# Causal attention steps of tiles 5+0, 4+1, 3+2, 6, 7, with both tiles of a step transposed by one VectorE instruction in two of three causal layers

## The chip, the cores and the metric

The kernel runs on one core of a Trainium2 chip. Five compute engines work beside each other, each with its own instruction stream: TensorE (PE, matrix products, with its weight loads shown apart as PEld), VectorE (DVE), ScalarE (ACT), GpSimd (POOL) and SyncE (SP), which here issues DMAs. They meet through semaphores; a wait at the head of an engine's stream holds everything behind it. TensorE writes to PSUM, a small memory of accumulators; the other data lies in SBUF, 128 partitions wide. The metric is the device time of one execution in microseconds, the median of several runs. A query tile is 128 rows.

## The reference, cut to what matters

Four transformer layers on x of 2 x 1024 x 128, each an attention and a feed-forward part with a layer norm ahead and a residual sum behind. All attentions have 16 heads of 64. Layer a has one key and value head shared by all and no mask; b, c and d are causal; c's keys and values come from a latent of 32 numbers per position; d has biases on its projections.

```python
def _L0_attn_b_ref(x, w_q, w_k, w_v, w_o):            # layer b; c and d alike but for what is said above
    q = jnp.einsum('bsd,hqd->bhsq', x, w_q)
    k = jnp.einsum('bsd,hqd->bhsq', x, w_k)
    v = jnp.einsum('bsd,hvd->bhsv', x, w_v)
    scores = jnp.einsum('bhsq,bhtq->bhst', q, k)
    causal = jnp.triu(jnp.ones((s, s), dtype=bool), k=1)
    masked = jnp.where(causal, -jnp.inf, scores)
    weights = jax.nn.softmax(masked / jnp.sqrt(jnp.float32(dq)), axis=-1)
    out = jnp.einsum('bhst,bhtv->bhsv', weights, v)
    cat = out.transpose(0, 2, 1, 3).reshape(b, s, -1)
    return jnp.einsum('bsf,df->bsd', cat, w_o)

x = x + attn_a(ln(x)); x = x + ffn(ln(x))             # ffn of a and b: dense, weight quantized to 6 bits
x = x + attn_b(ln(x)); x = x + ffn(ln(x))
x = x + attn_c(ln(x)); x = x + moe(ln(x))             # moe of c and d: top 2 of 8 experts, and a shared one
x = x + attn_d(ln(x)); x = x + moe(ln(x))
```

## The kernel before

**Units and steps.** The attention of a layer is cut into 16 units: a batch entry (2) and a pair of heads (8). A unit's 1024 queries are 8 tiles of 128 (NT). A step computes the scores of both heads for one query tile, or for two whose keys together fill the eight key tiles. In layer a a unit has 8 steps of one tile. In a causal layer tile qt has qt + 1 key tiles, and a unit has five steps, `CAUSAL_STEPS` (L588): [7], [6, 0], [5, 1], [4, 2], [3], of 8, 8, 8, 8 and 4 key tiles. So layer a has 128 steps, and b, c and d have 80 each. All steps of all units run one after another in one loop; the feed-forward parts, layer norms and the next unit's projections are cut in small parts and strewn between the steps.

**What one turn of the loop issues, in order.** The order on every engine is that of the text, written out by hand. For step s:

1. `transposes` (L764) for step s-2, the normalized probabilities of which are now ready. Before its second part, `normalize` (L702) for step s-1: DVE takes the reciprocals of the sums (L704), POOL multiplies (L708).
2. `add_products`: POOL adds finished output products to x (L894).
3. `scores` for step s: PE products into two PSUM tiles of two banks, one per head (L638), with the causal mask added by PE (L644 in b and d, L653 in c); DVE takes the negated row maxima (L682). `exponentials`: ACT, with the sums (L697). The two PSUM tiles are all there are, so a head's scores wait until ACT has read the same head's scores of the step before.
4. Copies queued by the transposes (ACT, L1146), then `out_product` (L864): PE's product with the output weights (L871) and ACT's copy out of PSUM (L878).
5. Parts of the next unit's projections (L533, L556, L571, their ACT copies, L541 in layer c, and in b and d the DMAs that swap the halves of q and k, L516) and of the side work.
6. `release` and `weigh_some(4)`: PE's products of up to four key tiles of transposed probabilities with the values (`weigh`, L850; c: L845, L841). They go into one PSUM tile `av` (the only one of its kind). When a bank of query tiles ends, ACT copies it to `attnT` (L861; d: L857).

**Two ways to transpose.** The products with the values need the probabilities with the keys on the partitions. The query tiles are taken in pairs, qb = qt // 2. In the first way (tiles 4 to 7 of a causal layer, and the first seven key tiles of all tiles in a) DVE transposes 32 x 32 blocks in place in each partition group (L778, STREAM_TRANSPOSE) from `pr` into `slots`. When both tiles of a pair are there, `blocks_moved` (L739) moves the sixteen blocks [quarter i of partitions, quarter r] of `slots` to their places in `prT`: 16 DMAs from SP's queue (L753); in layer a the diagonal ones need only change their place inside their own partitions and are copied, quarters 1 and 2 by POOL (L757) and 3 by ACT. In the second way (tiles 0 to 3 of the causal layers, the last key tile in a) PE transposes tiles of 128 x 128 into a PSUM tile `pp` of four (L794, from the pool `ps_m` of three buffers, which the projections and output products use too), and ACT copies them to SBUF (L795).

**Homes.** The transposed probabilities of a pair lie in a home: `prT_many[0]`, `prT_many[1]` or `prT_four` by their number of key tiles. `prT_of` (L713) takes it, and if products of an earlier pair that lies there are still to be issued, it issues them at once, at that place in the order. A pair becomes `ready` two steps after it was moved, or at once if PE transposed it; ready pairs are weighed in the order of `BANKS` (L590), in a causal layer [3], [0, 1], [2] (pairs), so a unit ends three banks.

Of the kernel before, what the change touches and what calls it, by code (L numbers as in the profile page):

```python
# [9 lines left out]
F32 = mybir.dt.float32  # L10
# [7 lines left out]
P = 128  # L18
B, S, D = 2, 1024, 128
NT = S // P  # L20
# [12 lines left out]
SCALE = 1.0 / 8.0  # L33


@with_exitstack
def kernel(ctx: ExitStack, tc: tile.TileContext, a: dict, out: bass.AP):
# [30 lines left out]
    def load_attn(names):  # L68
# [33 lines left out]
    slots = probTp.tile([P, 2, 2 * NT * AB], F32, tag="slots", name="slots")  # L102
    prT_many = [
        probTp.tile([P, 2 * NT * AB], F32, tag=f"prT{n}", name=f"prT{n}") for n in range(2)
    ]
    prT_four = probTp.tile([P, 2 * 4 * AB], F32, tag="prT_four", name="prT_four")
# [472 lines left out]
    def tag_of(u):  # L579
# [8 lines left out]
    CAUSAL_STEPS = [[7], [6, 0], [5, 1], [4, 2], [3]]  # L588

    BANKS = {  # L590
        "shared": [[0, 1], [2, 3]], "full": [[3], [0, 1], [2]], "latent": [[3], [0, 1], [2]],
        "bias": [[3], [0, 1], [2]],
    }

    BLOCKED = {"shared": (0, 1, 2, 3), "full": (2, 3), "latent": (2, 3), "bias": (2, 3)}
    HOMES = {8: "first", 6: "second", 4: "four", 2: "rest"}
    probT, pv_of, held = {}, {}, {}
# [4 lines left out]
    def blocked(u, qb):  # L602

        if qb not in BLOCKED[layers[u[0]]["kind"]]:
            return 0
        nk = keys(u, qb * TPA + TPA - 1)
        return nk if layers[u[0]]["causal"] else nk - 1
# [4 lines left out]
    def step_of(u, qts):  # L612
        k = f"{tag_of(u)}_{qts[0]}"
        at = {}
        if len(qts) == 2:
            at = {qts[1]: 0, qts[0]: keys(u, qts[1]) * P}
        else:
            at = {qts[0]: QB - min(QB, keys(u, qts[0]) * P // 2)}
        pr = probp.tile([P, NT, 2, P], F32, tag="pr", name=f"pr_{k}")
        tot = small.tile([P, 2, len(qts)], F32, tag="tot", name=f"tot_{k}")  # L620
        return dict(u=u, qts=qts, at=at, k=k, pr=pr, tot=tot)
# [66 lines left out]
    def tiles_of(st, qt):  # L688
        t0 = st["at"][qt] // P
        return st["pr"][:, t0 : t0 + keys(st["u"], qt)]  # L690
# [22 lines left out]
    def prT_of(u, qb):  # L713


        nk = keys(u, qb * TPA + TPA - 1)
        odd = nk == NT and qb % 2 and not layers[u[0]]["causal"]
        for part in ("second", "rest") if odd else (HOMES[nk],):
            old, held[part] = held.get(part), (u, qb)
            while old:  # L720
                if any(x[:2] == old for x in products):
                    weigh_some(4)
                elif any(x["key"] == old for x in late):
                    release()
                else:
                    break
        if odd:
            return prT_many[1]
        return {
            8: prT_many[0], 6: prT_many[1][:, : 12 * AB], 4: prT_four, 2: prT_many[1][:, 12 * AB :]  # L730
        }[nk]

    def blocks_of(u, qb):

        return slots[:, 1 - qb % 2, : 2 * blocked(u, qb) * AB]

    def blocks_moved(u, qb):  # L739


        t, src = prT_of(u, qb)[:, : 2 * blocked(u, qb) * AB], blocks_of(u, qb)
        n = src.shape[1] // 4
# [3 lines left out]


        copied = (1, 2, 3) if layers[u[0]]["kind"] == "shared" else ()
# [12 lines left out]
        probT[u, qb] = t.rearrange("p (i t k h q) -> p t h i k q", t=TPA, h=2, i=4, q=32)  # L762

    def transposes(st):  # L764

        u = st["u"]
        for qt in st["qts"]:
            qb, cols = qt // TPA, slice(qt % TPA * P, (qt % TPA + 1) * P)  # L770
            nk, nb = keys(u, qt), blocked(u, qb)
            tiles = tiles_of(st, qt)
            if nb:
                n = min(nk, nb)
                dst = blocks_of(u, qb).rearrange(
                    "p (r t c q) -> p t c r q", r=4, t=TPA, q=32
                )[:, qt % TPA, : 2 * n]
                nc.vector.transpose(  # L778
                    dst,
                    tiles[:, :n].rearrange("p k h (r q) -> p (k h) r q", q=32),  # L780
                )
                yield
            if nb < nk and nb:
                o = rest_of(u, qb)[:, qt % TPA].unsqueeze(2)
            elif nb < nk:
                if (u, qb) not in probT:
                    probT[u, qb] = prT_of(u, qb).rearrange("p (h k q) -> p h k q", h=2, q=AB)
                o = probT[u, qb][:, :, :, cols]
            for k0 in range(nb, nk, 2):
                k1 = min(k0 + 2, nk)  # L790
                pt = ps_m.tile([P, 2, 2, P], F32, tag="pm", name=f"pp_{tag_of(u)}_{qt}_{k0}")
                for h in range(2):
                    for kt in range(k0, k1):
                        nc.tensor.transpose(pt[:, h, kt - k0, :], tiles[:, kt, h, :], ident)  # L794
                nc.scalar.copy(o[:, :, k0 - nb : k1 - nb], pt[:, :, : k1 - k0, :])  # L795
                yield
            complete[u, qb] = complete.get((u, qb), 0) + 1
            if nb and complete[u, qb] == TPA:
                blocks_moved(u, qb)

    def rest_of(u, qb):

        held["four"] = u, qb
        return prT_four.rearrange("p (n t h q) -> p n t h q", t=TPA, h=2, q=P)[:, qb]

    def weigh(u, qb, bank, kt, ends):
# [11 lines left out]

        def moving(h, kt, t0, t1=TPA):
            if not blocked(u, qb):  # L820
                return probT[u, qb][:, h, kt, t0 * P : t1 * P]
            if kt >= blocked(u, qb):
                return rest_of(u, qb)[:, :, h]
            x = probT[u, qb][:, t0, h] if t1 - t0 == 1 else probT[u, qb][:, :, h]
            return x[:, :, kt] if t1 - t0 == 1 else x[:, :, :, kt]

        def shaped(o, t0, t1=TPA):
            if not blocked(u, qb):
                return o[:, t0 * P : t1 * P]
            if kt >= blocked(u, qb):  # L830
                return o.rearrange("p (t q) -> p t q", t=TPA)
            if t1 - t0 == 1:
                return o[:, t0 * P : t1 * P].rearrange("p (i q) -> p i q", q=32)
            return o.rearrange("p (t i q) -> p t i q", t=TPA, q=32)

        for h in range(2):
# [12 lines left out]
            else:  # L849
                nc.tensor.matmul(  # L850
                    shaped(av[ROWS[h], n], t0), lhsT=vs[u][:, kt, h, :], rhs=moving(h, kt, t0),
                    start=(kt == 0), stop=(kt == nkt - 1),
                )
# [110 lines left out]
    late = deque()  # L964
# [66 lines left out]


    nc.gpsimd.memset(slots[:, 0, 2 * (NT - 1) * AB :], 0.0)
# [56 lines left out]
    for step, (n, u, qts, i, total) in enumerate([*steps, *[(None, None, None, 0, 1)] * 4]):  # L1090
# [31 lines left out]
        if st:  # L1122
# [6 lines left out]
            for qb in {qt // TPA for qt in st["qts"]}:  # L1129
                if complete[st["u"], qb] == TPA:  # L1130
                    x = next(x for x in late if x["key"] == (st["u"], qb))
                    x["ready"] = step + (2 if blocked(st["u"], qb) else 0)
# [101 lines left out]
```

## Time and profile before

| | us |
|---|---|
| median of 3 runs (2292.64 to 2297.32) | 2293.26 |
| the profiled execution | 2291.09 |
| its span, from the first to the last recorded instruction | 2289.4 |
| PE busy | 2103.5 (92%) |
| DVE busy | 1691.4 (74%) |
| ACT busy | 1492.9 (65%) |
| POOL busy | 1294.1 (57%) |
| bytes moved by DMA | 320 MB, 140 GB/s on average |

The profile is one execution on the chip. An engine's busy time is the union of its instructions; PE's matrix products are pipelined, so the durations of single ones add up to more than their union, and a group's own busy time is given apart from the mean duration of one. A line of a group reads: line of the kernel, engine, operation, output <- inputs by the program's names, shapes and count; then the busy microseconds and the mean nanoseconds of one; then the idle time of the engine just before these instructions, and which engine's instruction ended it. The mean granted clock of TensorE in this execution was 0.971 of full speed. The four layers follow each other along the span, each with the feed-forward part of the layer before strewn into its steps, and the last feed-forward part stands alone at the end.

### The profile page before, as it was taken

Reading aid. Unit: us, or ns where it says so; the run is one execution under the profiler, and the core shown is the slowest. Engines: PE = TensorE matmul, PEld = TensorE weight load, DVE = VectorE, ACT = ScalarE, POOL = GpSimd, SP = SyncE. Lnnn points to the kernel's source line nnn. Section 1 sums busy time; section 2 is a strip of 40 time slices with the busy share of each in tenths; the row PEclk is TensorE's granted clock in tenths of the full one; section 3 lists DMA queues with packets and bytes.
Section 4 is the critical chain, followed back from the end, with each engine's and each line's share of the span. In section 5 each row is a group of like instructions: output and inputs, shape, how many; then the busy total and the mean of one; then the engine's idle time right before and its main releaser. Section 6 shows DMA issues by size and latency. Waiting matters only on the chain.

```text
span 2289.4 us, 43111 instructions
## 1 busy us (share of the span) xinstructions
PE 2103.5 (92%) x14833; PEld 1231.8 (54%) x14833; DVE 1691.4 (74%) x2375; ACT 1492.9 (65%) x3340; POOL 1294.1 (57%) x1723
## 2 busy tenths in 40 slices
PE   6999999999998999999997888888889999999986
PEld 2454444444445666666654444444455666656663
DVE  7978999999886876678668877766766656766544
ACT  5777777667865666666655566655666557666652
POOL 4757777668765555465546655555644446544441
PEclk9999999999999999999998899999999999999998
DMA  5666666556676666666655556644665556646450
GB/s 140 145 150 155 159 154 149 131 131 150 153 189 152 149 160 162 161 155 154 147 131 124 129 130 139 141 109 103 171 157 133 122 119 158 161 118 145 111 139 10
DMA packets 144632, 320.42 MB, mean 140 GB/s; under 512 B 48288, under 2 KB 58784, under 8 KB 144416
## 3 DMA queue, kind: packets, MB, share of 16 engines
q1 hardware_dynamic: 144416, 317.67, 58.8%
q8 instruction: 120, 1.97, 0.4%
q14 instruction: 96, 0.79, 0.1%
HBM read 10.27 MB, written 2.10 MB: 5 GB/s over the span
## 4 chain that ended last, share of the span: by engine, by line
PE 58%; DVE 12%; SPq 9%; POOL 6%; ACT 5%; DMA 5%; issue 5%; DVEq 0%; ACTq 0%; POOLq 0%
SPq L753 9%; PE sc_a L638 7%; PE av_a L850 7%; PE av_d L850 5%; PE sc_b L638 5%; PE av_b L850 4%; PE sc_d L638 4%; DVE slots L778 4%; DMA prT<-slots 4%; ACT pr_c L697 2%; PE sc_c L638 2%; POOL pr_a L708 2%; DVE nmax_d L682 2%; DVE nmax_c L682 2%; PE pp_d L794 2%
## 5 line engine op out<-in xcount | busy, mean ns | idle before, releaser
L708 POOL TENSOR_SCALAR pr_a<-pr_a,rec_a 128x1024 f32<-128x1024 f32 x256 | 284.1, 1122 | 189.3 <-DVE rec_a L704 183.4
L697 ACT ACTIVATE pr_a<-sc_a,nmax_a 128x1024 f32<-128x1024 f32 x256 | 283.2, 1111 | 162.5 <-DVE nmax_a L682 94.1
L708 POOL TENSOR_SCALAR pr_d<-pr_d,rec_d 128x1024 f32<-128x1024 f32 (+7 forms) x256 | 187.0, 748 | 265.9 <-DVE rec_d L704 265.9
L682 DVE TENSOR_REDUCE nmax_a<-sc_a 128x1 f32<-128x1024 f32 x256 | 300.0, 1212 | 49.7 <-PE sc_a L638 49.6
L708 POOL TENSOR_SCALAR pr_b<-pr_b,rec_b 128x1024 f32<-128x1024 f32 (+7 forms) x256 | 190.0, 760 | 216.0 <-DVE rec_b L704 215.8
L682 DVE TENSOR_REDUCE nmax_d<-sc_d 128x1 f32<-128x1024 f32 (+7 forms) x256 | 177.4, 750 | 173.0 <-PE sc_d L644 172.3
L708 POOL TENSOR_SCALAR pr_c<-pr_c,rec_c 128x1024 f32<-128x1024 f32 (+7 forms) x256 | 188.4, 754 | 195.7 <-DVE rec_c L704 195.7
L697 ACT ACTIVATE pr_c<-sc_c,nmax_c 128x1024 f32<-128x1024 f32 (+7 forms) x256 | 186.5, 739 | 146.2 <-DVE nmax_c L682 118.1
L697 ACT ACTIVATE pr_b<-sc_b,nmax_b 128x1024 f32<-128x1024 f32 (+7 forms) x256 | 186.6, 739 | 142.8 <-DVE nmax_b L682 102.8
L697 ACT ACTIVATE pr_d<-sc_d,nmax_d 128x1024 f32<-128x1024 f32 (+7 forms) x256 | 186.6, 739 | 131.6 <-DVE nmax_d L682 117.6
L778 DVE STREAM_TRANSPOSE slots<-pr_a 128x1792 f32<-128x1792 f32 x128 | 261.0, 2039 | 12.7 <-POOL pr_a L708 8.7
L638 PE MATMUL sc_a<-k_a,q_a 64*128 64x512 f32 x512 | 261.3, 629 | 1.7 <-ACT pr_a L697 1.7
L682 DVE TENSOR_REDUCE nmax_b<-sc_b 128x1 f32<-128x1024 f32 (+7 forms) x256 | 177.1, 749 | 111.6 <-PE sc_b L644 110.6
L638 PE MATMUL sc_a<-k_a,qx_a 64*128 64x512 f32 x512 | 258.6, 629 | 0.0
L682 DVE TENSOR_REDUCE nmax_c<-sc_c 128x1 f32<-128x1024 f32 (+7 forms) x256 | 177.3, 750 | 97.7 <-PE sc_c L653 97.7
L850 PE MATMUL av_a<-prT,v_a 128*64 128x256 f32 x1792 | 223.2, 388 | 3.7 <-DMA prT<-slots 1.4
L850 PEld LDWEIGHTS av_a<-prT,v_a 128*64 128x64 f32 x1792 | 121.1, 137 | 122.7 <-issue 70.2
L638 PE MATMUL sc_d<-k_d,q_d 64*128 64x512 f32 (+3 forms) x416 | 158.9, 494 | 0.3 <-ACT pr_d L697 0.3
L638 PE MATMUL sc_b<-k_b,q_b 64*128 64x512 f32 (+3 forms) x416 | 158.8, 494 | 0.0
L638 PE MATMUL sc_b<-kx_b,qx_b 64*128 64x512 f32 (+3 forms) x416 | 153.3, 488 | 0.1
L638 PE MATMUL sc_d<-kx_d,qx_d 64*128 64x512 f32 (+3 forms) x416 | 153.2, 488 | 0.2
L778 DVE STREAM_TRANSPOSE slots<-pr_b 128x2048 f32<-128x2048 f32 (+1 forms) x64 | 121.8, 1903 | 12.0 <-DMA prT<-slots 8.8
(408 smaller groups left out, 4765.1 us busy)
## 6 DMA issues: line engine op xcount, KB each, us to landing
prT<-slots SPq DMA_DIRECT2D x768, 128.0 KB, 2.3
prT<-slots SPq DMA_DIRECT2D x832, 112.0 KB, 2.2
prT<-slots SPq DMA_DIRECT2D x768, 96.0 KB, 2.1
qx_b<-q_b SPq DMA_DIRECT2D x32, 256.0 KB, 3.6
kx_b<-k_b SPq DMA_DIRECT2D x32, 256.0 KB, 3.6
qx_d<-q_d SPq DMA_DIRECT2D x32, 256.0 KB, 3.7
kx_d<-k_d SPq DMA_DIRECT2D x32, 256.0 KB, 3.5
x<-in_x SPq DMA_DIRECT2D x4, 256.0 KB, 3.8
```

Source lines behind the costliest of these rows:

```text
L638: yield nc.tensor.matmul(sc[h][:, at[qt] + k0 : at[qt] + k1], lhsT=q[r, qt * P : (qt + 1) * P], rhs=kk[r, k0:k1], start=True, stop=not dia ...
L682: nc.vector.tensor_reduce(out=nmax[:, n : n + 1], in_=sc[h][:, c], axis=AX.X, op=ALU.max, negate=True)
L697: nc.scalar.activation(tiles_of(st, qt)[:, :, h, :], sc[:, c].rearrange("p (k q) -> p k q", q=P), AF.Exp, bias=nmax[:, n : n + 1], accum_o ...
L708: nc.gpsimd.tensor_scalar(out=pt, in0=pt, scalar1=rec[:, h, n : n + 1], scalar2=1.0, op0=ALU.mult, op1=ALU.mult,)
L753: nc.sync.dma_start(out=o, in_=x)
L778: nc.vector.transpose(dst, tiles[:, :n].rearrange("p k h (r q) -> p (k h) r q", q=32),)
L794: nc.tensor.transpose(pt[:, h, kt - k0, :], tiles[:, kt, h, :], ident)
L850: nc.tensor.matmul(shaped(av[ROWS[h], n], t0), lhsT=vs[u][:, kt, h, :], rhs=moving(h, kt, t0), start=(kt == 0), stop=(kt == nkt - 1),)
```

## The change

The causal steps become [5, 0], [4, 1], [3, 2], [6], [7], of 7, 7, 7, 7 and 8 key tiles, and the banks of a causal layer [1, 2], [0, 3], two instead of three. A step's tiles now lie at the end of the first score bank and from there on, so that a step of 7 key tiles splits into 3 and 4.

`slots` and `prT` are two tiles each, of 21 and of 15 key-tile blocks (`HELD`). `groups_of` says which query tiles are moved together, and `group_of` finds a tile's group. In a the groups are the pairs, as before. In b and d tiles 1, 4, 0, 5, 2, 3 are group 0 (2+5+1+6+3+4 = 21 blocks) and 6, 7 group 1 (15), all transposed by DVE: the two tiles of a step, which lie beside each other in `pr` and in `slots`, by one instruction. A group is moved when its last tile is there, with 13 DMAs and the diagonal quarters 1 and 2 copied by POOL and 3 by ACT (`COPIED`). In c, tiles 4 and 5 (home 0) and 6 and 7 (home 1) are transposed by DVE, each on its own, and moved with 16 DMAs per pair, none copied; tiles 2, 3 and 0, 1 are transposed by PE into home 0 behind them (`natural`). `claim` takes the place of `prT_of`: in a causal layer it takes a home for a whole unit, and it issues the products that are still open of all that lies there.

Instruction counts, per layer:

| | before | after |
|---|---|---|
| b and d: PE transposes (L794) | 320 | 0 |
| b and d: DVE transposes, columns | 16 each of 2048, 1792, 1536, 1280 | 16 of 2048, 64 of 1792 |
| b and d: DMAs of the move | 512 | 416 |
| b and d: POOL copies of the move | 0 | 32 of 32x1344, 32 of 32x960 |
| b and d: ACT copies of the move | 0 | 16 of 32x1344, 16 of 32x960 |
| b and d: ACT copies of PE's transposes | 96 | 0 |
| c: PE transposes | 320 | 320 |
| c: DMAs of the move, columns | 256 of 1024, 256 of 768 | 256 of 704, 256 of 960 |
| b, c and d: copies of av, and of output products | 48 each | 32 each |

The score products keep their number and their sum of columns. Tile 0's and tile 1's first key block are no longer in an order that one instruction can read, so in b and d `weigh` takes them in two of 128 columns.

```diff
-    slots = probTp.tile([P, 2, 2 * NT * AB], F32, tag="slots", name="slots")
-    prT_many = [
-        probTp.tile([P, 2 * NT * AB], F32, tag=f"prT{n}", name=f"prT{n}") for n in range(2)
-    ]
-    prT_four = probTp.tile([P, 2 * 4 * AB], F32, tag="prT_four", name="prT_four")
+    slots, homes = (
+        [
+            probTp.tile([P, n * 2 * P], F32, tag=f"{what}{m}", name=f"{what}{m}")
+            for m, n in enumerate(HELD)
+        ] for what in ("slots", "prT")
+    )
...
-    CAUSAL_STEPS = [[7], [6, 0], [5, 1], [4, 2], [3]]
+    CAUSAL_STEPS = [[5, 0], [4, 1], [3, 2], [6], [7]]
...
-        "shared": [[0, 1], [2, 3]], "full": [[3], [0, 1], [2]], "latent": [[3], [0, 1], [2]],
-        "bias": [[3], [0, 1], [2]],
+        "shared": [[0, 1], [2, 3]], "full": [[1, 2], [0, 3]], "latent": [[1, 2], [0, 3]],
+        "bias": [[1, 2], [0, 3]],
...
+    def groups_of(kind):
...
+        length = [qt + 1 for qt in range(NT)]
+        if kind == "latent":
+            return [
+                dict(home=home, qts=qts, moved=base is None, len=length, base=base)
+                for home, qts, base in (
+                    (0, (4, 5), None), (1, (6, 7), None), (0, (2, 3), 11), (0, (0, 1), 18)
+                )
+            ]
+        return [
+            dict(home=home, qts=qts, moved=True, len=length)
+            for home, qts in ((0, (1, 4, 0, 5, 2, 3)), (1, (6, 7)))
+        ]
...
+    COPIED = {"shared": (1, 2, 3), "full": (1, 2, 3), "latent": (), "bias": (1, 2, 3)}
...
+    def claim(u, g):
+        key = u, g["home"] if layers[u[0]]["causal"] else g["qts"]
+        if held.get(g["home"], [None])[0] == key:
+            return
+        old = {
+            x for home, (k, qbs) in held.items() for x in qbs
+            if home == g["home"] or layers[u[0]]["causal"] and not layers[k[0][0]]["causal"]
+        }
+        qbs = {
+            qt // TPA for x in GROUPS[layers[u[0]]["kind"]] for qt in x["qts"]
+            if x is g or layers[u[0]]["causal"] and x["home"] == g["home"]
+        }
+        held[g["home"]] = key, {(u, qb) for qb in qbs}
+        while old:
+            if any(x[:2] in old for x in products):
+                weigh_some(4)
+            elif any(x["key"] in old for x in late):
+                release()
+            else:
+                break
...
     def transposes(st):
...
+        gs = [group_of(u, qt) for qt in qts]
+        joint = len(qts) == 2 and gs[0] is gs[1] and gs[0]["moved"]
+        for qt, g in zip(qts, gs):
+            nk, nb = keys(u, qt), g["len"][qt] if g["moved"] else 0
             tiles = tiles_of(st, qt)
+            if nb and not (joint and qt == qts[1]):
+                first = qts[1] if joint else qt
+                n = sum(g["len"][x] for x in qts) if joint else nb
...
+                src = st["pr"][:, st["pos"][first] : st["pos"][first] + n]
+                nc.vector.transpose(dst, src.rearrange("p k h (r q) -> p (k h) r q", q=32))
                 yield
...
             elif nb < nk:
...
+                claim(u, g)
+                o = natural(g)[:, g["at"][qt] : g["at"][qt] + nk]
...
+            count = complete[u, g["qts"]] = complete.get((u, g["qts"]), 0) + 1
+            if count == len(g["qts"]):
+                if g["moved"]:
+                    blocks_moved(u, g)
+                finished.append((u, g))
...
     def weigh(u, qb, bank, kt, ends):
...
+        in_blocks = g["moved"] and kt < g["len"][qb * TPA + TPA - 1]
+        whole = not in_blocks or at[1] > at[0]
...
+                for t in (t0,) if t0 or whole else range(TPA):
+                    ts = (t, TPA if whole else t + 1)
+                    nc.tensor.matmul(
+                        shaped(av[ROWS[h], n], *ts), lhsT=vs[u][:, kt, h, :],
+                        rhs=moving(h, kt, *ts), start=(kt == 0),
+                        stop=(kt == qb * TPA + ts[1] - 1 if causal else kt == nkt - 1),
+                    )
```

## The prediction

> **What bounds the kernel now.** I read first the table of stretches, cut where each layer's first score product starts (a from 21, b from 681, c from 1178, d from 1656, the last ffn from 2209 us); its columns are the stretch's length, each engine's busy time with its instructions, the granted clock and the DMA share.
>
> ```profile
> core 0: us, PE busy (x) PEld busy (x) DVE busy (x) ACT busy (x) POOL busy (x), PEclk, DMA share, GB/s
> 21.00:681.00 660.00, 628.74 (x3694) 303.99 (x3694) 591.74 (x613) 489.31 (x877) 459.89 (x475) 0.99 0.64 149
> 681.00:1178.00 497.00, 478.95 (x3643) 319.14 (x3643) 352.14 (x534) 322.93 (x804) 263.69 (x393) 0.99 0.65 154
> 1178.00:1656.00 478.00, 402.08 (x3306) 224.90 (x3305) 356.09 (x549) 303.03 (x777) 272.84 (x411) 0.93 0.55 130
> 1656.00:2209.00 553.00, 530.13 (x3892) 345.31 (x3893) 350.45 (x545) 352.98 (x843) 273.71 (x405) 1.00 0.58 138
> ```
>
> In b and d TensorE (PE) is busy 96% of the time, and VectorE (DVE) 71% and 63%: a product less there is time less. Layer c is another regime: PE 84%, DVE 74%, nothing full, so its pace is a chain of waits from engine to engine. Layer a, which the change leaves alone, shows both engines near full at once: PE 95%, DVE 90%. Second, the groups of instructions, where the change's own operations stand (count, busy us, mean ns, idle before):
>
> ```profile
> L778 DVE STREAM_TRANSPOSE slots<-pr_a 128x1792 f32<-128x1792 f32 x128 | 261.0, 2039 | 12.7 <-POOL pr_a L708 8.7 <-DMA prT<-slots 1.0 <-issue 0.2
> L778 DVE STREAM_TRANSPOSE slots<-pr_b 128x2048 f32<-128x2048 f32 x16 | 36.9, 2306 | 8.8 <-DMA prT<-slots 8.6
> L778 DVE STREAM_TRANSPOSE slots<-pr_b 128x1792 f32<-128x1792 f32 x16 | 32.5, 2033 | 0.3 <-POOL pr_b L708 0.2
> L778 DVE STREAM_TRANSPOSE slots<-pr_b 128x1536 f32<-128x1536 f32 x16 | 28.3, 1770 | 0.5 <-DMA prT<-slots 0.2 <-DMA kx_b<-k_b 0.2
> L778 DVE STREAM_TRANSPOSE slots<-pr_b 128x1280 f32<-128x1280 f32 x16 | 24.0, 1502 | 2.4 <-POOL pr_b L708 2.4
> L794 PE MATMUL pp_b<-ident,pr_b 128*128 128x128 f32 x320 | 49.6, 284 | 5.9 <-ACT attnT_b L878 3.1 <-POOL pr_b L708 2.6
> L794 PE MATMUL pp_d<-ident,pr_d 128*128 128x128 f32 x320 | 48.8, 284 | 4.3 <-POOL rc_n L328 1.9 <-POOL rc_m L328 1.9 <-POOL lnt_n L143 0.4
> L757 POOL TENSOR_SCALAR prT<-slots 32x896 f32<-32x896 f32 x128 | 121.4, 948 | 9.9
> L1146 ACT COPY prT<-slots 32x896 f32<-32x896 f32 x64 | 59.9, 936 | 1.6
> ```
>
> **Layers b and d: what goes.** All 320 PE transposes of each layer go: 49.6 and 48.8 us of PE's busy time. The score products keep their counts and columns. The attention products (av) get 64 narrow instructions more per layer for 32 wide ones, as tile 0's first key block no longer lies beside tile 1's; the trace holds each as two records, so by its rows (narrow 17.5 us per 180 = 0.097, wide 106.9 per 832 = 0.128) 128 x 0.097 - 64 x 0.128 = 4.2 us, and tiles 0 to 3 are now read in strips of 32, whose wide product averages 395 ns against 379: 2 us at most. I take 6 (0 to 8). PE's work is then 479 - 50 + 6 = 435 in b and 530 - 49 + 6 = 487 in d. Over PE's busy time stands an overhead: 497/479 = 1.04 in b, 553/530 = 1.04 in d, and 660/629 = 1.05 in a, where DVE is as full as it will be here. With a's factor b takes 456 (-41) and d 511 (-42); with their own, 452 and 507. I take a's for b and d's own for d, which keeps more spare DVE time: -41 and -46, -87 in all; from -58 (a third of it lost) to -105 (no added products, and the idle 5.9 and 4.3 before the transposes goes too).
>
> **What comes in its place, and what hides it.** DVE, per unit of five steps: four instructions of 2.04 and one of 2.31 for 2.31 + 2.03 + 1.77 + 1.50: 10.46 - 7.61 = 2.85 us more, 45.6 per layer, so 398 of 456 (87%) in b and 396 of 507 (78%) in d. A step of b then has 4.97 us of DVE in 5.7; layer a hides 591.74/128 = 4.62 in 5.16, so I cost it at nothing; without that cover it costs its 45 per layer. POOL gets two copies of 32x1344 and two of 32x960 per unit; at 948/896 ns per column that is 2 x 1.42 + 2 x 1.02 = 4.9 us, 78 per layer: 342 of 456 (75%; a: 70%). ACT loses six copies per unit (at least 26.6 us per layer for the 48 of 128x512) and one pair of output copies, and gets 1.40 + 1.00 us: about even. SyncE (SP) issues 26 DMAs per unit for 32, at some 0.63 us each (its issues in the chain of waits stand 0.6 apart): less. Group 0 is a burst of 13 x 172 KB = 2.2 MB; the fullest stretch of the trace (834 to 842 us) moved 226 GB/s, so 9.9 us and some 2.3 to land. It is issued in a unit's last step, behind the claim of its home, and first read at the end of the next unit's second step, some 14 us on: hidden, by 2 us. Group 1 (1.6 MB, 7.1 us) has as long. If group 0 were 2 us later, PE would wait 2 us per unit, 32 in each layer; one such loss lies within my lower bound of the gain.
>
> [...]
>
> **Layer c: what is moved.** Here tiles 0 to 3 stay with PE, but three things change. Their home is now shared with tiles 4 and 5, and the claim of it, when tile 0 is transposed (ahead of the unit's third scores in PE's order), forces out the products of the previous unit's tiles 0 and 1. These need the one PSUM tile of av, which ACT must empty first, and ACT's copy stands behind the step's exponentials and a projection copy:
>
> ```profile
> 1342.31 0.61 ACT L541 ACTIVATE q_c<-pq_c 128x512 f32<-128x512 f32 x1
> 1342.79 0.39 ACT L861 COPY attnT_c<-av_c 128x256 f32<-128x256 f32 x1
> 1341.15 1.13 PE L638 MATMUL sc_c<-latT,q_c 32*128 32x256 f32 x4 [0.93 <-ACT pr_c L697]
> ```
>
> (Start, duration, instruction, idle before and who ended it.) Before, the next scores start at 1341.15, as soon as the first head's exponentials are read, 1.2 us before ACT is through with the second's (1342.31). After, they wait for that, for 0.6 (q copy), 0.6 (a 128x512 attnT copy: 604 ns), about 0.5 of products (16 take 1.07 in the same timeline) and 0.2 of transposes. That is 3.1 us for the first head and 1.9 for the second; as the second head's scores start late now, I take the mean, 2.5 per unit. Next, the step [3,2] needs 14 PE transposes in four PSUM tiles where the pool has three, so the fourth waits for an ACT copy behind the exponentials; at a 0.6 us copy and the 0.6 it stands behind, 1.2 per unit. On the other side, PE's 27.9 us of waiting for POOL's normalization before these transposes (a row of the groups) came largely from the short step [3] running into the full one [7]; steps are now 7, 7, 7, 7, 8 wide, and I credit two thirds, -1.1 per unit. Sum 2.6 x 16 = +42; bounds 0 (the chain has that slack) and +59 (no credit).
>
> **The end.** The last step was tile 3 with four keys and PE transposes; now it is tile 7 with eight, a DVE transpose, 13 DMAs and their landing with nothing beside them. By 4 more score blocks per head (0.43 us each in nmax and exponentials) and 8 products more I put +4 (0 to +8) on the tail.
>
> **Sum.** 2291.1 (the profiled execution, 2289.4 of it the span) - 87 + 42 + 4 = 2250; the median of the runs stands 2.2 above the profiled execution, so 2252.
>
> **The rivals.** (1) c's chain absorbs the wait, as ACT is idle a third of that layer (303 busy of 478): 2252 - 42 = 2210. Against it: the step's loop passes through ACT's exponentials, and 118 us of ACT's idle is itself a wait in that loop, for the maxima. (2) The other side: DVE sets the pace in b and d. DVE waits 111 us in b and 172 us in d for the scores before it can take their maxima. If these waits stay, because scores wait for a free PSUM pair, which waits for exponentials, which wait for maxima, then the transposes are added in full: b 352 + 46 + 111 + 12 (transposes' own idle) = 521 (+24), d 350 + 46 + 173 = 569 (+16), with c and the tail 2293 + 24 + 16 + 42 + 4 = 2379. It decides as soon as DVE's work and waits pass 6.2 us a step in b and 6.9 in d. Against it: in a the same loop waits only 49.6 us in 128 steps, with more transposing. (3) The removed transposes half stood in gaps: in b's timeline eight records of them take 1.09 us, 0.136 each where the group's mean is 0.155, so some overlap other work; and the gain halves: 2252 + 43 = 2295, no change. Against it: PE's 96%. That the change leaves PE transposes in b and d is excluded by its text: both groups there are marked as moved by DMA.
>
> **How the numbers follow.** Main case 0.60, its own range 2220 to 2284 (b and d from -103 to -72, c from +25 to +58, tail 0 to +8, not all at their ends together). Rival 1 0.17, rival 2 0.13, rival 3 0.10. No change is within 0.2%, 4.6 us, which is about what a measurement of this kernel can tell. The main case and rival 1 are faster; of rival 3 I give 0.03 to faster, 0.04 to same, 0.03 to slower: faster 0.80, same 0.04, slower 0.16. The range takes in rival 1 and most of rival 3, and leaves rival 2 out: 2203 to 2299.
>
> **What would show it.** Right: no pp_b or pp_d group; b's stretch near 456 and d's near 507 with PE still over 93%; the 2.04 us transposes with little idle before them; in c a wait of av_c for ACT of some 2 us, sixteen times, and a stretch near 520. Wrong: DVE over 92% in b with PE's idle before sc_b (rival 2); av_b's first product waiting for prT<-slots by over 1 us per unit (group 0 late); c's stretch still near 478 (rival 1); b and d shortened by half of it with PE as full as before (rival 3).

## The result and the profile after

The changed kernel takes 2310.58 us (median of 4, 2307.93 to 2315.08) where the one before takes 2295.29 beside it: 1.007 times the time, 95% interval 1.0053 to 1.0087. It is slower; a gain of 41 us was forecast. The profiled execution has a span of 2309.2 us against 2289.4. The stretches of the changed kernel, cut as before at each layer's first scores (length, busy time of PE, its weight loads, DVE, ACT, POOL with the instructions, granted clock, DMA share, GB/s):

```profile
21.00:679.00 658.00, 625.22 (x3694) 303.15 (x3694) 590.44 (x610) 488.62 (x876) 458.74 (x475) 0.99 0.64 150
679.00:1158.00 479.00, 447.00 (x3388) 290.74 (x3388) 397.56 (x549) 315.63 (x713) 332.84 (x438) 0.98 0.67 163
1158.00:1685.00 527.00, 420.77 (x3312) 232.96 (x3310) 351.60 (x549) 302.29 (x740) 272.89 (x398) 0.89 0.47 112
1685.00:2221.00 536.00, 501.80 (x3610) 317.35 (x3608) 395.09 (x558) 341.19 (x746) 337.77 (x446) 0.98 0.59 145
2221.00:2309.20 88.20, 56.98 (x296) 35.42 (x293) 36.80 (x101) 21.86 (x36) 23.97 (x20) 0.78 0.20 50
```

| stretch | before | after | change | forecast |
|---|---|---|---|---|
| start and layer a | 681 | 679 | -2 | 0 |
| b | 497 | 479 | -18 | -41 |
| c | 478 | 527 | +49 | +42 |
| d | 553 | 536 | -17 | -46 |
| end | 80.4 | 88.2 | +8 | +4 |

So c lost about what was forecast, and b and d gained 35 us instead of 87. Of b's 49.6 us of PE transposes 32 left PE's busy time, and only 18 the time.

The new operations cost what their rows of before promised. The groups of the transposes in b, and of POOL's copies in d:

```profile
L810 DVE STREAM_TRANSPOSE slots<-pr_b 128x1792 f32<-128x1792 f32 x64 | 130.4, 2037 | 22.0 <-POOL pr_b L730 20.1 <-DMA prT<-slots 1.4 <-issue 0.2
L786 POOL TENSOR_SCALAR prT<-slots 32x1344 f32<-32x1344 f32 x30 | 39.1, 1304 | 3.6 <-PE av_d L886 1.4
```

The first takes 2037 ns, as in layer a, but DVE now stands idle 22 us before it, 20 of them behind POOL's normalization. DVE is 83% busy in b (87% was forecast, of a shorter stretch) and POOL 69%. The reader's question is where 46 us of DVE were paid for. Two stretches of four units each in layer b answer it: in the first only attention runs, in the second a feed-forward part is strewn between the steps, which shows in DVE's instructions. First the kernel before, then the changed one:

```profile
874.70:992.10 117.40, 116.19 (x897) 77.64 (x896) 78.84 (x120) 80.08 (x200) 61.15 (x92) 1.00 0.67 159
992.10:1117.30 125.20, 121.86 (x931) 81.62 (x931) 96.51 (x149) 82.15 (x205) 71.42 (x105) 1.00 0.65 155
```

```profile
830.20:938.90 108.70, 107.77 (x836) 70.35 (x834) 87.18 (x112) 79.35 (x178) 81.62 (x110) 1.00 0.75 183
938.90:1065.30 126.40, 113.34 (x864) 73.71 (x862) 108.80 (x156) 79.04 (x178) 85.98 (x112) 0.99 0.64 155
```

The quiet units go from 117.4 to 108.7 us, PE 99% busy in both: 2.2 us per unit less, close to the 2.6 of the forecast. The units with feed-forward work go from 125.2 to 126.4: nothing is gained. There DVE's share rises from 77% to 86% and PE's falls from 97% to 90%. The waits in b (engine and line, what it waited for, us, times, the longest) show the chain that took over:

```profile
ACT pr_b L719 <- DVE nmax_b L704: 141.4, 72, 6.6
...
PE sc_b L660 <- ACT pr_b L719: 21.2, 13, 5.0
```

Before, the first was 102.8 and the second did not stand among b's waits of PE at all: maxima come late, then exponentials, then scores.

### The profile page after: what moved, and what is told of

The parts are those of the page before. It is cut to its first block, busy times and chain, and to the rows that moved or that the text cites. A ratio compares the mean times of both kernels' runs of the same rounds, so it can differ in the third digit from the quotient of the medians.

```text
span 2309.2 us, 41731 instructions
## 1 busy us (share of the span) xinstructions
PE 2061.3 (89%) x14321; PEld 1185.2 (51%) x14321; DVE 1780.8 (77%) x2407; ACT 1474.8 (64%) x3116; POOL 1433.2 (62%) x1802
## 4 chain that ended last, share of the span: by engine, by line
PE 47%; DVE 15%; POOL 12%; ACT 8%; issue 8%; SPq 6%; DMA 4%; DVEq 0%; ACTq 0%; POOLq 0%
PE av_a L886 7%; PE sc_a L660 7%; SPq L782 6%; DVE slots L810 5%; ACT pr_c L719 4%; PE sc_b L660 4%; DMA prT<-slots 4%; PE sc_c L660 3%; DVE nmax_c L704 3%; PE av_b L886 3%; POOL pr_d L730 3%; PE sc_d L660 3%; PE av_d L886 2%; POOL prT L786 2%; POOL pr_b L730 2%
## 5 line engine op out<-in xcount | busy, mean ns | idle before, releaser
L730 POOL TENSOR_SCALAR pr_c<-pr_c,rec_c 128x768 f32<-128x768 f32 (+7 forms) x256 | 187.1, 748 | 242.9 <-DVE rec_c L726 242.9
L730 POOL TENSOR_SCALAR pr_d<-pr_d,rec_d 128x768 f32<-128x768 f32 (+7 forms) x256 | 186.5, 745 | 182.5 <-DVE rec_d L726 182.4
L719 ACT ACTIVATE pr_c<-sc_c,nmax_c 128x768 f32<-128x768 f32 (+7 forms) x256 | 186.5, 739 | 172.9 <-DVE nmax_c L704 158.0
L704 DVE TENSOR_REDUCE nmax_c<-sc_c 128x1 f32<-128x768 f32 (+7 forms) x256 | 177.2, 749 | 144.5 <-PE sc_c L675 144.4
L786 POOL TENSOR_SCALAR prT<-slots 32x896 f32<-32x896 f32 (+2 forms) x256 | 271.6, 1061 | 23.6 <-DVE slots L810 2.5
L719 ACT ACTIVATE pr_d<-sc_d,nmax_d 128x768 f32<-128x768 f32 (+7 forms) x256 | 186.6, 739 | 153.6 <-DVE nmax_d L704 148.5
L719 ACT ACTIVATE pr_b<-sc_b,nmax_b 128x768 f32<-128x768 f32 (+7 forms) x256 | 186.6, 739 | 151.6 <-DVE nmax_b L704 141.4
L730 POOL TENSOR_SCALAR pr_b<-pr_b,rec_b 128x768 f32<-128x768 f32 (+7 forms) x256 | 189.5, 757 | 133.6 <-DVE rec_b L726 132.3
L810 DVE STREAM_TRANSPOSE slots<-pr_a 128x1792 f32<-128x1792 f32 x128 | 260.9, 2038 | 11.7 <-POOL pr_a L730 7.5
L704 DVE TENSOR_REDUCE nmax_d<-sc_d 128x1 f32<-128x768 f32 (+7 forms) x256 | 176.7, 746 | 93.1 <-PE sc_d L666 92.8
L704 DVE TENSOR_REDUCE nmax_b<-sc_b 128x1 f32<-128x768 f32 (+7 forms) x256 | 176.5, 744 | 44.7 <-PE sc_b L666 44.5
```

Source lines behind the costliest of these rows:

```text
L704: nc.vector.tensor_reduce(out=nmax[:, n : n + 1], in_=sc[h][:, c], axis=AX.X, op=ALU.max, negate=True)
L719: nc.scalar.activation(tiles_of(st, qt)[:, :, h, :], sc[:, c].rearrange("p (k q) -> p k q", q=P), AF.Exp, bias=nmax[:, n : n + 1], accum_o ...
L730: nc.gpsimd.tensor_scalar(out=pt, in0=pt, scalar1=rec[:, h, n : n + 1], scalar2=1.0, op0=ALU.mult, op1=ALU.mult,)
L786: nc.gpsimd.tensor_scalar(out=o, in0=x, scalar1=1.0, scalar2=1.0, op0=ALU.mult, op1=ALU.mult)
L810: nc.vector.transpose(dst, src.rearrange("p k h (r q) -> p (k h) r q", q=32))
```

## The experiments

A table of all runs; b, c and d are the stretches of the profile, one execution each. They are cut at the first score product of a and c, the first masking product of b and d, and the last one of d, which moves b's and c's lengths by 1 us against a cut at the first scores alone. Stretches of the same code differ by up to 8 us between profiles in b (the changed kernel, e3, e5 and e14) and by 13 in c (522.7 in e4, 536.0 in e1), so less than that is not read from one stretch alone.

| run | ratio to before, 95% interval | b | c | d |
|---|---|---|---|---|
| before | 1 | 496.1 | 479.5 | 550.5 |
| changed | 1.007 (1.0053 to 1.0087) | 477.7 | 528.2 | 535.0 |
| e1 no copies | 1.0047 (1.0033 to 1.0061) | 478.9 | 536.0 | 522.8 |
| e2 separate | 1.0047 (1.0027 to 1.0067) | 474.4 | 530.3 | 531.0 |
| e3 c in the old order | 0.9987 (0.9975 to 0.9999) | 476.2 | 508.9 | 536.9 |
| e4 order alone | 1.0363 (1.034 to 1.0387) | 510.1 | 522.7 | 570.8 |
| e5 c's banks | 0.9999 (0.9987 to 1.0012) | 483.8 | 514.3 | 531.9 |
| e6 old order, DVE | 1.023 (1.0202 to 1.0258) | 504.9 | 501.9 | 567.0 |
| e7 all by DVE | 0.9874 (0.9855 to 0.9893) | 478.2 | 488.0 | 529.8 |
| e9 more DVE | one time, 2333.4 us | 493.7 | 526.1 | 542.2 |
| e11 more PE | one time, 2358.4 us | 505.9 | 521.5 | 560.1 |
| e12 spread in b and c | 0.9873 (0.9855 to 0.989) | 467.4 | 495.9 | 531.2 |
| e13 more PE in c | 0.9905 (0.989 to 0.992) | 476.1 | 494.6 | 532.2 |
| e14 three PSUM tiles | 0.9982 (0.9964 to 1.0) | 481.6 | 510.9 | 531.9 |
| e15 before, more DVE | one time, 2319.3 us | 507.8 | 492.6 | 555.4 |
| e16 spread in b alone | 0.9843 (0.9816 to 0.987) | 468.0 | 489.4 | 533.1 |

**What holds b and d back.** Four runs change one part each of b and d. e1, without the diagonal copies:

```diff
-    COPIED = {"shared": (1, 2, 3), "full": (1, 2, 3), "latent": (), "bias": (1, 2, 3)}
+    COPIED = {"shared": (1, 2, 3), "full": (), "latent": (), "bias": ()}
```

> The changed kernel with the diagonal blocks of b and d moved by DMA (16 instead of 13 per group), so that POOL loses its 4.9 us and ACT its 2.4 us of copies per unit. Theory A (POOL's copies stand ahead of the normalization, so DVE's transposes, the maxima, the exponentials and the scores come late): the stretch of b falls from 479 to 469 or less and d's from 536 to 526 or less, POOL near 256 busy in b, whole near 2290. Theory B (the new order of steps costs by itself: unequal pieces of the score products, steps that are all 7 wide, PE's work unevenly spread): b and d stay within 4 us of 479 and 536; the three more DMAs per group are hidden.

b did not move and d fell by 12, more than the 5 by which d differs between the changed kernel, e3, e5 and e14; the whole may be 2 per mille better, with overlapping intervals. POOL's copies are not b's cause; in d they may be a part of it. e2, a transpose for each tile:

```diff
-        joint = len(qts) == 2 and gs[0] is gs[1] and gs[0]["moved"]
+        joint = False
```

> The changed kernel with one DVE transpose per tile in place of one per step in b and d: 3 more instructions per unit, some 0.27 us of fixed time each (1770 - 1502 ns for 256 columns is 1.05 ns a column, so 1502 - 1280 x 1.05 = 0.16 to 0.27 us fixed), 13 us of DVE per layer at most. If the wait of a joint transpose for the second tile's normalization (some 1.2 us, 25 us of DVE idle before transposes in each layer) matters, b and d fall by 5 to 15 us each; if DVE's own time sets the pace, they rise by 5 to 13 each; if neither, within 3.

b and d are 3 and 4 us shorter, within the scatter; one instruction for two tiles gains nothing. e4 keeps the new order but lets PE transpose as in c, with homes, moves and claims as there (stretches from a second execution, 2374.2 us; the ratio is of the other runs):

```diff
-        if kind == "latent":
+        if kind != "shared":
```

> The new steps, banks and homes in all causal layers, but b and d transpose tiles 0 to 3 with PE as c does, and move (4,5) and (6,7) by 16 DMAs: the order of the steps without the joint DVE transposes. If the order costs nothing in a layer that PE bounds, b and d are at the old 497 and 553 within 6, whole near 2345 (497 - 479 + 553 - 536 = 35 over the changed one). If it costs by itself (theory B), b and d are above these by 15 to 45 us each, whole 2375 to 2435, and the gain from the DVE transposes is larger than the whole change shows.

With PE's transposes the new order costs b 14 and d 20 us against before, 34 in all where 25 to 30 were expected of the second execution; the DVE transposes then bring 32 and 36. But this is not the price of the order alone. e4's waits of PE in b begin with the forced products of c (told below), 12.1 us of them in d too:

```profile
PE av_b L886 <- ACT attnT_b L898: 13.3, 14, 2.0
```

The changed kernel does not have this wait among b's waits of PE, so nearly all of e4's 14 us in b can be a wait that comes with PE's transposes in shared homes, and says little of the changed kernel. What the order does cost there is PE time of the scores, 166.1 us in b before and 178.6 after, which the forecast did not have. e4 has 169.5, so the new pieces make 3.4 of these 12.5; the rest appears only with the DVE transposes, where scores start after waits. The first row is the changed kernel's, the second e4's, for the same product:

```profile
L660 PE MATMUL sc_b<-k_b,q_b 64*128 64x448 f32 x160 | 82.8, 604 | 3.7 <-ACT pr_b L719 3.7
```

```profile
L660 PE MATMUL sc_b<-k_b,q_b 64*128 64x448 f32 x160 | 79.3, 582 | 0.4 <-ACT pr_b L719 0.4
```

Where it waits more the product is slower, 604 ns against 582, and b's granted clock is 0.98 against 1.00 in e4. e6 goes the other way, the old order and its three banks with the DVE transposes:

```diff
-    CAUSAL_STEPS = [[5, 0], [4, 1], [3, 2], [6], [7]]
+    CAUSAL_STEPS = [[7], [6, 0], [5, 1], [4, 2], [3]]
...
-            for home, qts in ((0, (1, 4, 0, 5, 2, 3)), (1, (6, 7)))
+            for home, qts in ((0, (0, 2, 4, 1, 5, 3)), (1, (6, 7)))
```

> The old steps [7], [6,0], [5,1], [4,2], [3] and three banks in all causal layers, with b and d transposed by DVE alone (the two tiles of [5,1] and [4,2] by one instruction, 2048 columns each), moved as tiles 0 to 5 and 6, 7 as in the changed kernel; c as before. If the order is what cost the gain (theory B): the scores' PE time in b returns from 178.6 to 166, b's stretch is 460 or less, d's 515 or less, c's 480 to 495, whole near 2225. If the DVE transposes themselves hold b and d back (POOL's and DVE's load): b stays within 6 of 478 and d of 535, whole 2250 to 2265. A third possibility: group 0 is moved one step later than in the changed kernel and its slots are refilled two steps after, so DVE waits for the DMAs (more than 1 us per unit), and b is slower than 490.

It is slower than both kernels, though not by the wait for DMAs (8.8 us in 7 waits, not 1 per unit). So theory B, that the new order spoils the gain, falls for the DVE transposes. Why the old order suits them so badly was not followed further; in e6's b PE also waits 20.9 us, 28 times, for the copy of av ahead of the output products, against 1.5 us in the changed kernel.

That left the pace itself, and two runs put weight on one engine at a time: e9 on DVE, e11 on PE, both in every causal step. Neither result is used.

```diff
+        if st and layers[st["u"][0]]["causal"]:            # e9, after the transposes
+            nc.vector.tensor_reduce(
+                out=spare[:, :1], in_=m_gate, axis=AX.X, op=ALU.max, negate=True
+            )
...
+        if new and layers[u[0]]["causal"]:                 # e11, at the end of the step
+            for t in range(4):
+                nc.tensor.transpose(pt[:, t, :], ident, ident)
```

> The changed kernel with one more DVE instruction of some 0.68 us (a maximum over 128x512 of a constant) in each causal step, 3.4 us per unit, so that the suspected cost is about doubled; the result is not used. Theory D (DVE sets the pace of b's units in which layer a's or b's feed-forward work is strewn, PE that of the others): the units with such work, 31 to 34 us now, become 2.5 to 3.5 us longer; the four quiet units in the middle, 27.2 us now, less than 1.5 longer, as DVE is free there 1.08 us a step; b in all 478 + 20 to 40. Rival (PE's own work and its lower clock set the pace throughout): b under 478 + 12 in all, busy and quiet units alike.

> The changed kernel with four more PE transposes of the identity (some 0.55 us, 2.7 per unit) at the end of each causal step; nobody reads them. Theory D: b's quiet units become 2 to 3 us longer (PE is 99% busy there), the units with feed-forward work less than 1.2 (PE is idle 10% there), b in all 478 + 12 to 22; in c, where PE waits, the granted clock rises from 0.89 to 0.93 or more and c grows by less than 8 or falls. Rival (PE sets the pace throughout): all units of b 2 to 3 us longer, b 478 + 40.

e15 puts e9's instruction into the kernel before:

> The kernel before with one more DVE instruction of some 0.68 us in each causal step (54 us per layer, against the 46 that the change adds) and nothing removed. If the prediction's term was right (DVE's added time lies beside PE's), b and d stay within 3 of 496 and 550. If DVE is already on the path in the units with feed-forward work (theory D), b grows by 10 to 25 us, in those units alone, the quiet ones by less than 0.5 each; c, where the changed kernel took no harm from it (526 against 528), within 8.

The length of b's units, as means of the four quiet ones and of the next four with feed-forward work (from one full-width exponential to the next):

| us per unit | quiet | with feed-forward work |
|---|---|---|
| before | 29.4 | 31.3 |
| before, DVE +3.3 (e15) | 29.5 | 32.3 |
| changed | 27.2 | 31.6 |
| the same b in e3, e5 and e14 | 27.0 to 27.2 | 32.1 to 33.0 |
| changed, DVE +3.3 (e9) | 27.3 | 33.6 |
| changed, PE +2.5 (e11) | 29.5 | 32.6 |

In quiet units the answer is clear: DVE's 3.3 us are free and PE's 2.5 are paid with 2.3, where the same code differs by 0.2. With feed-forward work it differs by 1.4 between profiles, so DVE's 3.3 are paid with 0.6 to 2.0 and PE's 2.5 with 1.0 at most: PE does not set the pace alone there, but the two shares are not settled. That DVE was on the path even before the change shows in e15's sums. Its whole time, 2319.3 us, lies 16 above the highest of 13 executions of the kernel before beside it (2285.1 to 2303.2, median 2295.2); of the 11.7 us by which b grew, the four quiet units hold 0.5, the four after them 4.0 and the six ahead of them 7.3. c grew by 13 there, where 8 at most was expected, and d by 5; this is no more than the same code scatters in the changed kernel. In all, on the changed kernel, b rose by 16 for 43 us more of DVE's busy time and by 28 for 40 of PE's; d by 7 (within the scatter) for 44 and by 25 for 35. Theory D's sizes were too large for DVE (16 where 20 to 40 was expected) and too small for PE (28 for 12 to 22), but the sides are right in quiet units.

If the feed-forward work decides where DVE counts, then spreading it must help without a single instruction less. e12 lowers the rate of the side work in b and c, e16 in b alone, both on e7 (below):

```diff
-    SIDE = [1.1, 1.5, 2.8, 2.8]
+    SIDE = [1.1, 1.2, 2.3, 2.8]                            # e12; e16: [1.1, 1.2, 2.8, 2.8]
```

> Layer c by DVE too, one instruction per tile (as in the run of all three layers by DVE), with the side work's rate lowered in b from 1.5 to 1.2 parts a step and in c from 2.8 to 2.3, so that more units share it. Theory D: b falls from 478 to 470 or less, c by a few us, whole near 2255. Rival: the sum of waits is the same wherever the side work lies, b within 4 of 478 and the whole within 6 of 2266.

> Layer c by DVE too, one instruction per tile, with the side work's rate lowered in b alone (1.5 to 1.2 parts a step). If the run with b and c lowered lost in c what it won in b (b 478 to 467, c 488 to 496), b is at 467 and c at 488 again, whole near 2256; if the two are coupled, the whole stays within 3 of 2266.

b fell from 478 to 467 and 468, with the same instructions on each engine. The feed-forward work of all engines is spread by this, so it does not name DVE alone. With the lower rate in c too the whole is 2265.61 us, no less than e7's 2265.86, where 2255 was expected; e16 is the fastest kernel here: 2259.25 us, 0.9843 of before (0.9816 to 0.987).

**What c lost.** The forecast's mechanism stands in the timeline of the changed kernel (start, duration, instruction, idle before and its end), in a unit without other work:

```profile
1337.53 0.61 ACT L543 ACTIVATE q_c<-pq_c 128x512 f32<-128x512 f32 x1
1338.01 0.60 ACT L898 COPY attnT_c<-av_c 128x512 f32<-128x512 f32 x1
...
1338.67 0.64 PE L879 MATMUL av_c<-prT,lat_c 128*32 128x256 f32 x2 [2.46 <-ACT attnT_c L898]
...
1339.69 0.69 PE L822 MATMUL pp_c<-ident,pr_c 128*128 128x128 f32 x2
...
1351.68 0.44 PE L822 MATMUL pp_c<-ident,pr_c 128*128 128x128 f32 x2 [1.32 <-ACT prT L823]
```

PE stands 2.46 us until ACT has copied q and then emptied the PSUM tile of av, and only then come the forced products, tile 0's transposes and the scores; 12 us later the last tile of step [3,2] waits 1.32 for a PSUM tile. c's waits of PE sum these up:

```profile
PE av_c L879 <- ACT attnT_c L898: 38.4, 15, 5.3
...
PE pp_c L822 <- ACT prT L823: 9.9, 11, 1.3
PE po_c L908 <- DMA wo_c<-c_wvo: 6.6, 1, 6.6
```

e5 removes the first by another order of the banks, with homes claimed pair by pair instead of by the whole unit:

```diff
-        "latent": [[1, 2], [0, 3]]
+        "latent": [[0, 1], [2, 3]]
...
-        key = u, g["home"] if layers[u[0]]["causal"] else g["qts"]
+        key, lo = (u, g["qts"]), g.get("base") or 0
```

> The changed kernel with layer c's banks as [0,1], [2,3] in place of [1,2], [0,3], and homes claimed pair by pair: tiles 0 and 1 are weighed in the unit's last steps and not forced out ahead of the next unit's third scores; the new steps stay. Theory C1 (the forced products behind ACT's attnT copy are most of c's loss): the 38 us of PE waiting for attnT_c at av_c go below 8, c's stretch falls from 528 to 490 or less, whole near 2270. Theory C2 (the four PSUM tiles of step [3,2] and the 7-wide steps are most of it): the wait goes, but c stays above 510, as PE then waits for POOL's normalization or for the exponentials in its place.

The 38.4 are gone, but c is at 514, above the 510 of theory C2. Its own waits of PE:

```profile
PE sc_c L660 <- ACT pr_c L719: 23.7, 29, 1.6
PE pp_c L818 <- POOL pr_c L730: 20.1, 21, 3.7
PE po_c L904 <- DMA wo_c<-c_wvo: 13.1, 1, 13.1
...
PE pp_c L818 <- ACT prT L819: 0.9, 3, 0.4
```

Waits for POOL's normalization take up 15 of what was won (20.1 after 4.8), and a single wait for the output weights 6.5 more, as the first products come earlier. The second wait, of PE's transposes for a PSUM tile, has fallen with the first, from 9.9 to 0.9. e14 goes on from e5 with steps that need at most three PSUM tiles:

```diff
+    LATENT_STEPS = [[5, 0], [4, 2], [3, 1], [6], [7]]
```

> As the run with c's banks [0,1], [2,3], and c's steps as [5,0], [4,2], [3,1], [6], [7] (7, 8, 6, 7, 8 wide), so that no step needs more than three PSUM tiles for PE's transposes. If the fourth tile's wait for ACT is what is left of c's loss (1.2 us per unit), c falls from 514 to 495 or less and the quiet units from 28 to below 27; if the 7-wide steps as such cost it, c stays within 6 of 514.

The four quiet units fell from 28.0 to 26.9 us (changed: 29.9, before: 26.2), the whole of c only from 514 to 511, within the scatter, where 495 was expected. So in quiet units the two runs bring back 3.0 of the 3.7 us lost, but with only 0.9 us of the wait for a fourth tile left in all of e5's c, e14's 1.1 are not that wait; by what they come is not shown. In the units with feed-forward work some 2 us per unit remain; 9 us of these are the one wait for the output weights (12.9 after 3.8 before), and the cause of the rest was not found. e3 puts c back to the old steps and banks, its homes claimed pair by pair:

```diff
+    LATENT_STEPS = [[7], [6, 0], [5, 1], [4, 2], [3]]
```

> The changed kernel with layer c alone put back to the old steps [7], [6,0], [5,1], [4,2], [3] and the old three banks, its homes taken for each pair by itself; b and d as changed. Theory C (c's loss of 49 us is the order of its steps, with the forced products and the four PSUM tiles of one step): c's stretch from 527 back to 478 within 8, the waits of av_c for ACT's attnT copy from 38 to under 8 us, whole near 2262. Rival: c lost by the layout of its homes or by its uneven moves (704 and 960 columns), which stay: c's stretch above 505, whole above 2285.

c came to 509, not 478. But 17.6 us of that are one unit: the first of c took 44.6 us instead of 27.0, where b in the new order meets c in the old one and b's open products are forced out at once (PE waited 9.2 us for attnT_b there). Without it c is at 491, still outside the 8 us that theory C allowed, but 37 of the 49 us are gone with the order. e7 lets DVE transpose in c too, in all three layers without joint instructions, and copies c's diagonal blocks as in b:

```diff
-        if kind == "latent":
+        if kind == "never":
...
-            for home, qts in ((0, (1, 4, 0, 5, 2, 3)), (1, (6, 7)))
+            for home, qts in ((0, (0, 1, 2, 3, 4, 5)), (1, (6, 7)))
```

> The new steps, with tiles transposed by DVE alone in c too, one instruction per tile, tiles 0 to 5 in their own order (so that tile 0 and 1 are read in one piece): c then has no PE transposes, no PSUM tiles of them and no forced products. If c's loss came with PE's transposes in the new order, c falls from 528 below 475 (56 us of PE transposes and their waits go, 45 us of DVE come) and the whole to 2255 or less; if the 7-wide steps themselves are slow in a layer that runs as a chain of waits, c stays above 500.

c falls to 488, not below 475, and the whole beats both kernels. The stretch of c in e7:

```profile
1157.90:1645.90 488.00, 400.93 (x2999) 206.88 (x2998) 405.60 (x614) 298.82 (x678) 345.48 (x460) 0.87 0.55 134
```

PE has 54 us of transposes less than in either kernel, and is still busy 401 us where before it was 403: its granted clock is 0.87 where it was 0.93. e13 tries to hold the clock with PE work that nobody reads, e11's transposes in c alone, on e7:

> Layer c by DVE too, as in the run of all three layers by DVE, with four more PE transposes of the identity at the end of each step of layer c alone, which nobody reads. If the half-clock stretches of c (granted clock 0.87 on average) lengthen its chain, the clock rises above 0.93 and c falls from 488 to 478 or less although PE has 44 us more to do. If not, c stays within 5 or grows by 5 to 20.

The clock rose to 0.91 only, c went from 488 to 495, and the whole grew by 7, from 2265.86 to 2273.01 us. In e11, on the changed kernel, c's clock rose from 0.89 to 0.95, and c did not grow (521.5 after 528.2) though it has 80 times four transposes more: there they cost no more than the scatter, and PE's busy time rose by 15 us only.

## Why the prediction was wrong

The step that failed is "so I cost it at nothing; without that cover it costs its 45 per layer": DVE's added time in b and d. The cover was read from averages, 4.97 us of DVE in a step of 5.7, and from layer a, where DVE is as full. But layer b is two regimes, and the average of a layer says nothing of either. In its quiet units DVE's time was indeed free, and the gain 2.2 us per unit, near the 2.6 forecast. In those with feed-forward work nothing was gained, and DVE's time was being paid for before the change: e15 adds 0.66 us of it to each causal step, 43 to 46 us of busy time per layer, and takes 24 us more in all, b 11.7 more, nearly none of that in quiet units. This is the forecast's second rival, in half of the layer only; its condition, DVE's work and waits over 6.2 us per step, was worked out for the whole layer and so looked far off. An estimate from the measured prices has the direction and half of the size: PE's busy time fell by 32 in b and 28 in d, at 0.7 us per us (e11) -22 and -20; DVE's rose by 45, at 0.27 to 0.37 in b and 0.11 to 0.16 in d (e15, e9) +12 to +17 and +5 to +7; sum -10 to -5 and -15 to -13, against -18 and -17 measured. In b it falls 8 to 13 us short of the gain; PE's price may have been higher before, when it was fuller, which was not measured. In d DVE's price lies within the scatter, so there the step is not shown: what is known is that less left PE than forecast, and that the copies may have a part.

A second, smaller step: "The score products keep their counts and columns" was taken to mean their time. PE's time of the scores rose by 12.5 us in b and 10.7 in d, 3.4 of b's by the pieces (e4); the rest came with the waits ahead of them and a lower clock, and was not divided between these. So 32 and 28 us left PE instead of 44 and 43.

Point by point. PE transposes gone from b and d: right. av's added instructions, forecast at 6: they cost nothing, 141.6 against 140.1 us of PE time in b. b near 456 and d near 507 with PE over 93%: wrong, 479 and 536; PE is at 93% and 94%, but only because it is slower. DVE transposes with little idle before them: wrong, 22 us in b, behind POOL. Group 0's DMAs hidden: right, PE waited 0.5 us for prT in all of b. A transfer of 168 KB took 3.3 us to land where 2.3 was assumed, without harm. POOL and ACT, costed at nothing: right in b (e1), not settled in d. c's forced products: right in mechanism and place, 15 waits of 2.6 us. That c's +49 lies near the +42 is in part luck: the terms of the forecast measured 38.4 for these waits, 9.9 for the PSUM tile and 23.1 less of waiting for POOL, 25 in all, and the rest is mostly PE's own busy time, 19 us more at a granted clock of 0.89 after 0.93, which the forecast did not have. Beside POOL's copies the transposes took no longer: the 80 of b took 2010 to 2312 ns, the range of their two sizes alone (2010 to 2047 and 2278 to 2312), and the 28 of them that ran beside a POOL copy no more than 2047; in a before the change, with POOL busy 460 of 660 us, the 128 of 1792 columns took 2011 to 2047. Some other DVE instructions of b, which the forecast left out, did: of the changed kernel's 32 instructions of 128x512 with two inputs in the feed-forward part, none took more than 693 ns with POOL idle, and some up to 1674 with POOL at work beside them. The 32 took 25.1 us before and 30.4 after, in the very units where DVE's time counts; over the whole span their kind went only from 55.3 to 56.8. The end cost 8, forecast 4.

## What to carry to other kernels

When work is moved from the full engine to one that looks free, look at the new engine's share in each stretch of different side work, not over the layer: a mean of 83% was 80% in the units where DVE's time was free and 86% in those where nothing was gained. Before the move, add an unused instruction of the same length to that engine: one run gives its price, unit by unit, as far as units of the same code agree. And when buffers are shared by larger groups, ask what the claim forces out at that place of the order and which single PSUM tile stands in its way.

## What the runs showed of the hardware

Part of a gain in PE's work was given back in layer c. PE's granted clock there was 0.93 before, 0.89 in the changed kernel and 0.87 in e7, and unused transposes raised it, to 0.95 on the changed kernel (e11) and 0.91 on e7 (e13). PE's busy time in c was 403 and 401 us with and without 54 us of transposes, as the products of c's scores, the same in number, took 149.7 us before, 157.2 in the changed kernel and 176.8 in e7; how much of this is the clock was not separated. The clock did not go by PE's busy share alone: 80% with 0.89 in the changed kernel, 82% with 0.87 in e7, 79% with 0.92 in e9. The clock records of layer c before and in the changed kernel are all a half or one, and the half comes in pieces of 3.4 us or multiples of it. It makes 72 us of c before, 113 in the changed kernel, 130 of 487 in e7 and 55 in e11, in line with the granted clocks of 0.93, 0.89, 0.87 and 0.95.
